# Output weights prepared block by block behind contexts, query weights prepared at projection borders, and a later start of the three-head query lead

## The chip, the cores and the metric

The kernel runs on one core of a Trainium2 chip. A core has five engines that run side by side, each with a queue of its own that it works off in order: TensorE (PE in the profile; PEld are its weight loads, which overlap its matmuls), VectorE (DVE), ScalarE (ACT), GpSimd (POOL) and SyncE (SP), which here only issues DMAs. Engines wait for one another through semaphores. The metric is the device time of one execution in microseconds (us); a kernel's time is the median of its runs.

## The reference

The input is x with 4 sequences of 512 tokens and 1024 features, all in fp32. Four residual layers follow, each after a layer norm: a mixing across sequences, a linear layer with routed low-rank additions, a low-rank attention with 32 heads, and a linear layer with sequence-routed low-rank additions. The change concerns only the attention, which for one sequence is

```
q   = rmsnorm(x @ wq_a.T) @ wq_b.T            -> 32 heads x (64 plain + 64 rotary)
ckv, k_pe = split(x @ wkv_a.T)                -> 64 shared values, 64 rotary ones
k_nope, v = split(rmsnorm(ckv) @ wkv_b.T)     -> per head 64 and 128
scores = ([q_nope, rope(q_pe)] . [k_nope, rope(k_pe)]) * scale, causal
out = softmax(scores) @ v                     -> 32 heads x 128
y   = out @ wo.T                              -> 1024
x   = x + y
```

## The kernel before

**Stages.** By the profile's time, the first two layers fill 0 to 330 us, the low-rank projections of the attention 330 to 421 us, the heads 421 to 1496 us, and the last projection and the last layer the rest. The change lies in the heads.

**fp32 products.** The kernel splits each fp32 operand of a large product into a high part (a rounded copy, made by ACT or DVE) and a low part (the remainder, a subtraction by DVE or POOL) and adds three products: low by high, high by low, high by high (`matmul3`, lines 150 to 152). An operand thus always exists as a pair h, l.

**Units.** The keys and values are kept in the 64-wide shared form, so that the per-head key and value weights are folded into the query weights and the output weights. A unit u is one head of one sequence: 128 units, in 4 groups of 8 heads; within a group the 4 sequences follow one another, 8 heads each. One pass of the loop at line 1215 handles these things of different units:

- `query` of unit u+3: six 512-column matmuls into the one PSUM bank `psq`; `rotate_query`: ACT copies it to `qf` (L729), DVE makes the two rotated halves (L731, L732), POOL multiplies and adds (L733, L734);
- `split_query` of unit u+1: DVE rounds the high part `qh` (L741), POOL makes the low part `ql` (L742);
- `scores` of unit u: four pieces of 512, 384, 256 and 128 columns; the first three need `qh` and `ql`. DVE masks each and takes a minimum (L919), ACT takes the exponential (L922);
- `turn` of unit u-1: ten transposes of the probabilities on PE (L943), evicted by ACT and DVE (L945);
- `context` of units u-3 and u-2, in every second pass: sixteen profiled matmuls into `psv` (L959). Their results have 64 rows, so that two of them run side by side on PE;
- a few steps of a filler (the counts `per`): for the first sequence of a group `prepare_output`, otherwise `project` of the sequence before.

**Output weights.** Per group, `prepare_output` folds `wo` with the value weights. A block n is one pair of heads; its two halves of 512 columns are two PSUM tiles `poa` and `pob` (one buffer each), each made by two 64-row matmuls (L1069) from `slotC`, one buffer that `fetch_output` loads anew for each block (L1047, L1049). The projection runs as a two-by-two scheme of seven products (Strassen, in Winograd's form): of each two blocks seven operands are made, b11, b21, b22 and t1 to t4, each with a high part by ACT (`high`, L1083) and a low part by DVE or POOL (`low`, L1092 and L1089), with copies out of PSUM (`kept`, L1078) and differences (`less`, POOL L1096 or DVE L1099) in between. The copies lie in slices of the tile `raw`, of which there is one, shared with the loads of the query weights. Per group these are 24 operations on ACT, 16 on DVE and 6 on POOL. `issue_after` tells the scheduler to place a step behind a named instruction.

**Query weights.** A group has two sets, of four heads each. `fetch_query` loads the raw weights, in five DMAs on SP's queue, in the passes of heads 0 and 4 of a group's last sequence; `prepare_query` (L683, L684, L688, L145, L146) makes the pairs from them: four matmuls in `pob`, two copies on ACT, one subtraction on DVE and one on POOL. It is called in the middle of a pass, for the first set at head 3 of that last sequence and for the second at head 0 of the next group:

```
if (b, i) == (NB - 1, 3) and g + 1 < NG:
    wqs[2 * g + 2] = prepare_query(wq_raw, pso, "pob")
if (b, i) == (0, 0) and g > 0:
    wqs[2 * g + 1] = prepare_query(wq_raw, pso, "pob")
if u + 3 < NU:
    query(u + 3, psq, "psq")
    rotate_query(u + 3)
```

**Order.** The program is written in the order above, and the tile framework's scheduler then merges the steps into one fixed queue per engine. At run time each queue is worked off in that order, whatever is ready.

## Time and profile before

| | us |
|---|---|
| median of three runs | 1746.12 |
| the three runs | 1748.56, 1744.06, 1746.12 |
| profiled execution | 1748.5 |
| its span in the profile | 1746.3 |
| PE busy | 1704.6 |
| DVE, ACT, POOL busy | 1305.6, 903.5, 925.3 |
| span, 437.7 to 521.5 (group 0's output weights) | 83.8, of which PE busy 81.5 |
| mean of one `high` (L1083), `low` on DVE (L1092), `low` on POOL (L1089) | 0.60, 0.69, 1.29 |
| mean of one L733 or L734 on POOL, one L742 | 1.29, 1.02 |

The profiled execution is the slowest of the three. The page gives busy times of each engine over the span; a row of the timeline gives a start, a duration, the engine, the line, what is written and read, and in brackets how long the engine had sat idle and what released it. Because matmuls are pipelined, the time between the starts of two matmuls is the price of the first, not its own duration.

### The profile page before, as it was taken

The page shows a single profiled execution, that of the slowest core. Times are in us where ns is not written, and L with a number is a line of the kernel's source. Part 1 is how long each engine was busy: PE and PEld are TensorE (multiplying, and loading weights), DVE is VectorE, ACT ScalarE, POOL GpSimd, SP SyncE. Part 2 cuts the span into 40 slices and gives each one's busy share as a digit, 9 for nine tenths or more (in the row PEclk, how much of TensorE's full clock was granted, in tenths as well). Part 3 has the DMA queues.
Part 4 walks back from the last instruction along what each step waited for, and adds up shares of the span by engine and source line. Part 5 has one row for each costly group of instructions (what it writes and reads, how often), then busy time and mean ns, then how long its engine had stood idle before and what let it go on. Part 6 is the DMA issues. An engine that isn't in the chain of part 4 may idle for free.

```text
span 1746.3 us, 31729 instructions
## 1 busy us (share of the span) xinstructions
PE 1704.6 (98%) x10536; PEld 1432.1 (82%) x10536; DVE 1305.6 (75%) x3494; ACT 903.5 (52%) x2316; POOL 925.3 (53%) x926
## 2 busy tenths in 40 slices
PE   7999999999999999999999999999999999999999
PEld 6899999998767777767787767778777877789998
DVE  7977885676877777787777677777778777687675
ACT  7422331365765565475555476555466555453332
POOL 0553541202666565666666656666556664675454
PEclk9999999999999999999999999999999999999999
DMA  5313543245324234353333353242344333853431
GB/s 194 134 42 116 183 161 114 89 137 166 103 92 140 97 108 148 98 175 113 113 126 105 113 183 116 97 148 94 130 159 156 108 101 121 308 199 123 138 110 68
DMA packets 131940, 228.17 MB, mean 131 GB/s; under 512 B 22272, under 2 KB 58752, under 8 KB 128448
## 3 DMA queue, kind: packets, MB, share of 16 engines
q1 hardware_dynamic: 131776, 226.13, 38.7%
q8 instruction: 84, 1.38, 0.3%
q14 instruction: 80, 0.66, 0.1%
HBM read 156.60 MB, written 71.83 MB: 131 GB/s over the span
## 4 chain that ended last, share of the span: by engine, by line
PE 85%; DVE 7%; DMA 3%; ACT 2%; POOL 2%; issue 2%; SPq 0%; DVEq 0%; ACTq 0%; POOLq 0%
PE psv L959 8%; PE pst L943 8%; PE pss L150 4%; PE po L150 4%; PE po L152 4%; PE po L151 4%; PE pss L151 4%; PE pss L152 4%; PE pob L150 3%; PE psq L150 3%; PE poa L150 3%; PE psq L151 3%; PE psq L152 3%; PE pob L152 3%; PE pob L151 3%; PE acc L150 3%
## 5 line engine op out<-in xcount | busy, mean ns | idle before, releaser
L922 ACT ACTIVATE p<-p,mn 128x512 f32<-128x512 f32 (+3 forms) x512 | 284.6, 558 | 218.6 <-DVE mn L919 214.3
L919 DVE CUSTOM_DVE_ANT_0 p<-pss,causal 128x512 f32<-128x512 f32 (+3 forms) x512 | 232.4, 486 | 29.1 <-PE pss L152 21.9
L733 POOL TENSOR_TENSOR qf<-qf,ropeT 64x512 f32<-64x512 f32 x128 | 164.5, 1285 | 167.1 <-ACT qf L729 165.1
L943 PE MATMUL pst<-ident,p 128*128 128x128 f32 x1280 | 186.1, 273 | 3.7 <-ACT pT L945 3.7
L734 POOL TENSOR_TENSOR qf<-qf,wA 64x512 f32<-64x512 f32 x128 | 164.5, 1285 | 31.2 <-DVE wA L732 24.8
L943 PEld LDWEIGHTS pst<-ident,p 128*128 128x128 f32 x1280 | 153.0, 141 | 31.1 <-ACT pT L945 8.2
L742 POOL TENSOR_TENSOR ql<-qf,qh 128x384 fp32r<-128x384 f32 x128 | 131.1, 1024 | 63.9 <-DVE qh L741 47.6
L994 POOL TENSOR_TENSOR cxl<-s,cxh 128x256 fp32r<-128x256 f32 x128 | 96.8, 764 | 119.0 <-ACT cxh L993 65.1
L945 ACT COPY pT<-pst 128x512 f32<-128x512 f32 x256 | 142.4, 578 | 23.3 <-PE pst L943 21.3
L150 PE MATMUL pss<-kT,ql 128*128 128x512 f32 (+2 forms) x384 | 144.0, 375 | 0.8 <-DVE mn L919 0.4
L150 PE MATMUL po<-w_h,hTl 128*128 128x384 f32 (+1 forms) x384 | 133.1, 347 | 0.8 <-DVE x L433 0.8
L151 PE MATMUL pss<-kT,qh 128*128 128x512 f32 (+2 forms) x384 | 131.5, 342 | 0.0
L152 PE MATMUL pss<-kT,qh 128*128 128x512 f32 (+2 forms) x384 | 130.4, 340 | 0.0
L152 PE MATMUL po<-w_h,hTh 128*128 128x384 f32 (+1 forms) x384 | 130.1, 339 | 0.0
L151 PE MATMUL po<-w_l,hTh 128*128 128x384 f32 (+1 forms) x384 | 129.7, 338 | 0.0
L945 DVE COPY pT<-pst 128x256 f32<-128x256 f32 x128 | 54.3, 424 | 94.2 <-PE pst L943 93.1
L729 ACT COPY qf<-psq 128x512 f32<-128x512 f32 x126 | 74.0, 587 | 71.7 <-PE psq L152 71.7
L731 DVE TENSOR_TENSOR wA<-psq,ropeT 32x512 f32<-32x512 f32 x126 | 87.7, 696 | 22.5 <-ACT qf L729 19.5
L994 POOL TENSOR_TENSOR cxl<-cx,cxh 128x256 fp32r<-128x256 f32 x96 | 73.7, 769 | 55.6 <-ACT cxh L993 53.1
L922 ACT ACTIVATION_READ_ACCUMULATOR p<-p,mn 128x1 f32 x512 | 96.9, 189 | 0.0
L150 PEld LDWEIGHTS pss<-kT,ql 128*128 128x128 f32 x384 | 72.6, 189 | 21.9 <-DVE mn L919 4.3
L732 DVE TENSOR_TENSOR wA<-psq,ropeT 32x512 f32<-32x512 f32 x126 | 87.0, 691 | 1.7
(511 smaller groups left out, 4979.1 us busy)
## 6 DMA issues: line engine op xcount, KB each, us to landing
xs<-x_d SPq DMA_DIRECT2D x128, 256.0 KB
x_d<-xs SPq DMA_DIRECT2D x128, 256.0 KB
slotC<-in_woT_dram SPq DMA_DIRECT2D x32, 512.0 KB
rb<-r_d SPq DMA_DIRECT2D x128, 128.0 KB
w_t<-raw SPq DMA_DIRECT2D x32, 288.0 KB
x<-in_x_dram SPq DMA_DIRECT2D x16, 512.0 KB
x_d<-x SPq DMA_DIRECT2D x32, 256.0 KB
slotA<-q_d SPq DMA_DIRECT2D x8, 1024.0 KB
```

Of the source, the lines that this page charges most:

```text
L150: T.matmul(ps, lhsT=al, rhs=bh, start=start, stop=False, **kw)
L151: T.matmul(ps, lhsT=ah, rhs=bl, start=False, stop=False, **kw)
L152: T.matmul(ps, lhsT=ah, rhs=bh, start=False, stop=stop, **kw)
L733: G.tensor_tensor(f[mid], f[mid], ropeT[mid, 0, :], ALU.mult)
L734: G.tensor_tensor(f[mid], f[mid], t2[mid], ALU.add)
L742: G.tensor_tensor(l, f[:, P:S], f32(h), ALU.subtract)
L919: turn_of[0] = V.tensor_tensor_reduce(out=to, in0=ps[:, 0:n], in1=causal[:, S - n : S], scale=1.0, scalar=-NEG, op0=ALU.add, op1=ALU.min, ...
L922: A.activation(to, to, AF.Exp, bias=mn[:, i : i + 1], scale=-1.0, accum_out=rs[:, i : i + 1])
L943: T.transpose(ps[:, w : w + P], p[:, OF[i] + j * P : OF[i] + (j + 1) * P], ident)
L945: copy(pT[:, AT[js[0]] : AT[js[0]] + w], ps[:, 0:w])
L959: T.matmul(ps[n * KVR : (n + 1) * KVR, S - w : S], lhsT=k[:, j, :], rhs=pTs[u + n][:, AT[j] : AT[j] + w], start=(j == 0), stop=(j == TPB - 1))
L994: G.tensor_tensor(l, src, f32(h), ALU.subtract)
```

## The change

**Blocks.** `block(n)` makes both halves of a block at once, in both PSUM tiles, and loads the next block after it. The 22 steps of a group are written anew as 24, six in the stretch from a block to the next within a pair and six behind it, with two more differences kept in the free slices 4 and 5 of `room`. `less` goes to POOL whenever both sources lie in SBUF. Group 0 has an order of its own: 20 operations on ACT, 8 on DVE and 14 on POOL, where later groups have 16, 14 and 8. The counts of filler steps per pass (`per`) change so that a block follows a context.

**Query weights.** `fetch_query`'s result goes to a list, and `project` prepares it at the start of each half of a projection, with the bank that this half does not yet use.

**Queries.** Up to unit `EXTRA` = 12, a pass makes `query(u + 2)`, not `query(u + 3)`, and `split_query(u + 1)` comes after the first steps of the scores. In pass 12 both queries, of units 14 and 15, are made; from then on the order is that of before.

```diff
@@ -1014,6 +1014,9 @@
                             splitter(cxp, HG // 4, "cx"))
             parts = [next(outs), next(outs)]
             for j in range(0, TPB, 2):
+                if fetched_q:
+                    n, fetched = fetched_q.pop(0)
+                    wqs[n] = prepare_query(fetched, pso, "po" + "ab"[(1 + j // 2) % 2])
                 at, xs, banks = {}, {}, {}
                 for t, k in ((0, 0), (1, 1), (0, 1), (1, 0)):
                     at[t, k] = x_d[b * TPB + j + t][k]
@@ -1060,15 +1063,16 @@
             prs = [c + k for c in range(HG // 4) for k in (0, HG // 4)]
             po, tiles = {}, {}
 
-            def block(n, half, at):
+            def block(n):
                 nonlocal fetched
                 wo, wv = fetched
-                po[at] = pso.tile([P, 512], F32, name="po" + at)
                 with ExitStack() if g else tc.issue_after(scored[0].ins):
-                    for k in range(2):
-                        T.matmul(po[at][k * KVR : (k + 1) * KVR, :], lhsT=wv[:, k, :],
-                                 rhs=wo[k][:, half * 512 : half * 512 + 512], start=True, stop=True)
-                if half and n + 1 < len(prs):
+                    for half, at in enumerate("ab"):
+                        po[at] = pso.tile([P, 512], F32, name="po" + at)
+                        for k in range(2):
+                            T.matmul(po[at][k * KVR : (k + 1) * KVR, :], lhsT=wv[:, k, :],
+                                     rhs=wo[k][:, half * 512 : half * 512 + 512], start=True, stop=True)
+                if n + 1 < len(prs):
                     fetched = fetch_output(g, prs[n + 1])
 
             def src(at):
@@ -1092,89 +1096,66 @@
                     V.tensor_tensor(l, src(at), f32(h), ALU.subtract)
 
             def less(to, a0, a1):
-                if not {to, a0, a1} & set(po):
+                if not {a0, a1} & set(po):
                     G.tensor_tensor(src(to), src(a0), src(a1), ALU.subtract)
                     return
                 with tc.issue_after(turn_of[0].ins):
                     V.tensor_tensor(src(to), src(a0), src(a1), ALU.subtract)
 
             def steps():
-                block(0, 0, "a")
-                yield
-                kept(0, "a")
-                high("b11", "a")
-                block(0, 1, "b")
-                yield
-                low("b11", "a")
-                kept(1, "b")
-                yield
-                less("b", "b", 0)
-                block(1, 0, "a")
-                yield
-                high("t1", "b")
-                kept(0, "b")
-                kept(2, "a")
-                high("b21", "a")
-                yield
-                low("t1", "b")
-                low("b21", "a")
-                block(1, 1, "b")
-                yield
-                high("b22", "b")
-                kept(3, "b")
-                yield
-                low("b22", 3)
-                less("b", "b", 0)
-                block(2, 0, "a")
-                yield
-                high("t2", "b")
-                kept(5, "a")
-                less(3, 3, 1)
-                yield
-                low("t2", "b")
-                less("b", 2, "b")
-                high("b11", "a")
-                yield
-                high("t4", "b")
-                high("t3", 3)
-                low("b11", "a")
-                yield
-                low("t4", "b")
-                low("t3", 3)
-                block(2, 1, "a")
-                yield
-                kept(1, "a")
-                yield
-                less("a", "a", 5)
-                block(3, 0, "b")
-                yield
-                high("t1", "a")
-                kept(5, "a")
-                kept(2, "b")
-                high("b21", "b")
-                yield
-                low("t1", "a")
-                low("b21", "b")
-                block(3, 1, "a")
-                yield
-                high("b22", "a")
-                kept(3, "a")
-                yield
-                low("b22", 3)
-                less("a", "a", 5)
-                yield
-                high("t2", "a")
-                less(3, 3, 1)
-                yield
-                low("t2", "a")
-                less("a", 2, "a")
-                high("t3", 3)
-                yield
-                high("t4", "a")
-                low("t3", 3)
-                yield
-                low("t4", "a")
-                yield
+                for n in (0, 2):
+                    block(n)
+                    yield
+                    kept(1, "b")
+                    yield
+                    high("b11", "a")
+                    less(4, 1, "a")
+                    yield
+                    low("b11", "a")
+                    yield
+                    high("t1", 4)
+                    yield
+                    low("t1", 4)
+                    yield
+                    block(n + 1)
+                    yield
+                    if g == 0:
+                        kept(3, "b")
+                        less(5, "b", 4)
+                        high("b21", "a")
+                        yield
+                        kept(2, "a")
+                        high("b22", 3)
+                        low("b21", "a")
+                        yield
+                        high("t2", 5)
+                        low("b22", 3)
+                        less(3, 3, 1)
+                        low("t2", 5)
+                        yield
+                        high("t3", 3)
+                        less(2, 2, 5)
+                        low("t3", 3)
+                        yield
+                    else:
+                        less(5, "b", 4)
+                        high("b22", "b")
+                        yield
+                        low("b22", "b")
+                        less(2, "a", 5)
+                        high("b21", "a")
+                        yield
+                        less(3, "b", 1)
+                        low("b21", "a")
+                        high("t2", 5)
+                        yield
+                        low("t2", 5)
+                        high("t3", 3)
+                        low("t3", 3)
+                        yield
+                    high("t4", 2)
+                    low("t4", 2)
+                    yield
 
             return steps()
 
@@ -1211,7 +1192,9 @@
                     nc.sync.dma_start(out=tiles[t][:, k * 512 : (k + 1) * 512], in_=x_d[2 * q + t][k])
 
         filler = None
+        fetched_q = []
         cx = None
+        EXTRA = 12
         for u in range(NU + 3):
 
 
@@ -1219,12 +1202,12 @@
             g, b = divmod(B, NB)
             if i == 0 and B > 0:
                 filler = project(*divmod(B - 1, NB))
-            per = ((4, 1, 0) if i % 2 else (1, 1, 0)) if b else (2 + (i < HG // 2 + 2), 2, 2) if i >= HG // 2 else (3, 3, 1)
+            per = ((4, 1, 0) if i % 2 else (1, 1, 0)) if b else (2, 2, 2) if i >= HG // 2 else (3, 3, 1)
             if B == 0:
-                per = (0, 1, 2)
+                per = (1, 1, 1)
             if b == 0 and i == (HG // 2 if g else 0) and g < NG:
                 filler = prepare_output(g, wo_raw)
-            if u + 1 < NU:
+            if EXTRA < u < NU - 1:
                 split_query(u + 1)
             sc = scores(u) if u < NU else iter(())
             tn = turn(u - 1) if 0 < u <= NU else iter(())
@@ -1234,10 +1217,11 @@
             advance(sc)
             advance(cx)
             advance(filler, per[0])
+            if u <= EXTRA:
+                split_query(u + 1)
 
             if u == 0:
                 query(2, psq, "psq")
-                rotate_query(2)
             advance(sc)
             advance(sc)
             advance(tn)
@@ -1245,15 +1229,18 @@
             advance(filler, per[1])
             if u < NU:
                 g, b, i = units[u]
-                if (b, i) == (NB - 1, 3) and g + 1 < NG:
-                    wqs[2 * g + 2] = prepare_query(wq_raw, pso, "pob")
-                if (b, i) == (0, 0) and g > 0:
-                    wqs[2 * g + 1] = prepare_query(wq_raw, pso, "pob")
-            if u + 3 < NU:
+            if 0 < u <= EXTRA:
+                query(u + 2, psq, "psq")
+            if u <= EXTRA:
+                rotate_query(u + 2)
+            if EXTRA < u < NU - 3:
                 query(u + 3, psq, "psq")
                 rotate_query(u + 3)
             advance(filler, per[2])
             advance(tn)
+            if u == EXTRA:
+                query(u + 3, psq, "psq")
+                rotate_query(u + 3)
             if u < NU:
                 g, b, i = units[u]
                 if i == 2 and u + HG < NU:
@@ -1262,7 +1249,8 @@
                 if b == 0 and i == 0:
                     wo_raw = fetch_output(g, 0)
                 if (b, i) in ((NB - 1, 0), (NB - 1, 4)) and g + 1 < NG:
-                    wq_raw = fetch_query(2 * g + 2 + i // 4)
+                    n = 2 * g + 2 + i // 4
+                    fetched_q.append((n, fetch_query(n)))
                 if (g, b) == (NG - 1, NB - 1) and i == 1:
                     late = raw()
                     hs = {0: [late[:, (t + 1) * D : (t + 2) * D] for t in range(2)]}
```

## The prediction

> **What bounds the kernel now.** I read, in this order, the busy line of the page, the groups of instructions, the waits of the tensor engine in the stretches that the change touches, and there the rows in order of time. A difference counts when it is over 0.3% (5.2 us); less can't be told from no change here. The busy line first:

> ```profile
> PE 1704.6 (98%) x10536; PEld 1432.1 (82%) x10536; DVE 1305.6 (75%) x3494; ACT 903.5 (52%) x2316; POOL 925.3 (53%) x926
> ```

> PE is busy 98% of the span, so time is lost only where PE gets more to do or waits; no other engine is near full over the span. PE's waits in group 0's output weights (437 to 522 us, where all of group 0's part of the change lies), and then in the same work of the later groups (700 to 1420 us):

> ```profile
> engine line waited for: us in total, times, longest us
> PE pst L943 <- ACT pT L945: 2.2, 1, 2.2
> ```

> ```profile
> PE pst L943 <- ACT pT L945: 1.5, 3, 0.5
> PE pob L150 <- POOL cxl L994: 0.9, 3, 0.3
> PE poa L1069 <- DMA slotC<-in_wv_dram: 0.6, 1, 0.6
> ```

> So there is 2.25 us to win in group 0, and 3.0 us over the three later groups, 1.0 each. What the first wait stands behind is seen in ACT's rows in order of time (start, duration):

> ```profile
> 492.92 0.62 ACT L1083 CAST t31h<-raw 128x512 fp32r<-128x512 f32 x1 [2.48 <-POOL raw L1096]
> 493.45 0.72 ACT L922 ACTIVATE p<-p,mn 128x512 f32<-128x512 f32 x1
> ```

> One ACT copy waited 2.48 us for one subtraction on POOL, and the exponentials of the next head, queued behind it, came late to the transposes. An output-weight operation thus costs time by standing in a queue ahead of something that the scores need. That is what to look for in the new order. The last rows are POOL's own, for one query in this stretch, and what lies around it:

> ```profile
> 479.61 1.01 POOL L742 TENSOR_TENSOR ql<-qf,qh 128x384 fp32r<-128x384 f32 x1 [2.49 <-DVE qh L741]
> 481.15 1.28 POOL L733 TENSOR_TENSOR qf<-qf,ropeT 64x512 f32<-64x512 f32 x1 [0.52 <-ACT qf L729]
> 482.58 1.29 POOL L734 TENSOR_TENSOR qf<-qf,wA 64x512 f32<-64x512 f32 x1 [0.16 <-DVE wA L732]
> 484.78 1.02 POOL L742 TENSOR_TENSOR ql<-qf,qh 128x384 fp32r<-128x384 f32 x1 [0.91 <-DVE qh L741]
> ```

> The last three are one query: its matmuls ended at 480.3, and its low part was there at 485.8, 5.5 us later, with only its own three POOL operations in the queue. Its head's first scores start at 493.6, 13 us after its matmuls, so nothing is lost before the change.

> **Part 1, blocks in both halves.** PE's instructions are the same set; only their order differs, from 437.7 to about 520 us and in three like stretches later. Rows give: a whole context (16 matmuls into 64 rows, side by side in pairs) 2.30 us (488.36 to 490.66); a context with two block halves in it 4.14 (458.76 to 462.90), so 1.84 for two halves; one half alone 1.01 to 1.08; the first pair of a split context alone 1.00 (498.49 to 499.49) and its rest 2.29. Group 0 before: five halves alone (5.05), two whole contexts (4.6), two with halves (4.14 + 4.20), one split (3.29), one more whole (2.30): 23.6 us. After: one whole context with both halves (4.0), five first pairs alone (5.0), three rests with both halves (12.0), two rests (4.6): 25.6. **+2.0 us**: blocks become cheaper, but three contexts more are cut in two. At each later group the same count gives +0.63 for the block stretch, -0.65 for a context that becomes whole, -0.1 for query weights behind a context: -0.1.

> Evictions in group 0: ACT 24 to 20 (0.60 us each), DVE 16 to 8 (0.69), POOL 6 to 14 (1.29). Later groups: ACT 24 to 16, DVE 16 to 14, POOL 6 to 8. ACT and DVE get lighter by 2.4 and 5.5 us, POOL heavier by 8 x 1.29 = 10.3 us in group 0's two pairs of blocks. POOL is the engine that also makes the queries. The 2.25 us wait goes: the subtraction that ACT waited for is a different one now, and no exponential stands right behind it: **-2.3**.

> **Part 2, query weights moved.** Per set: 4 matmuls (0.9 us of PE), two ACT copies (0.62, 0.58), one DVE (0.69) and one POOL operation (1.28). All move from inside heads 0 and 3 to the two starts of a projection's half. They stay beside PE work of several heads, and the sets are used no sooner than before; if that cover goes, PE waits up to the 3.2 us of their chain. Their five loads on SP's queue keep their place in the head loop, but now some stand ahead of the load for a block (512 KB x2, 5.7 us alone, wanted about 7 us after its issue): 0 to 1 us of wait. At each later group I take the old wait of 1.0, less the -0.1 of matmul order, less 0.4 for what may come back: **-0.7** each, bounds -1.1 and +0.9; times three, -2.1.

> **Part 3, the additional query in the thirteenth head.** In the first twelve heads the query is now made two heads ahead instead of three, so its low part has to be ready one head after its matmuls, not two. For the query of head 7 I follow the new queues with the rows above; zero is the end of the block of pair 1. PE: last scores of head 5 and eight transposes (1.5), six query matmuls to 2.95; then two transposes 0.2, first scores of head 6 1.2, three transposes 0.3, scores 0.4, five transposes 0.5, first pair of the context 1.1, query 8 with one score 1.7, two transposes 0.2: scores of head 7 are wanted at about 8.8, 5.8 us after the query. The bare chain needs 5.5. But POOL's order is now: low part of head 6's query, a subtraction, b22's low part, first rotation of query 7, a subtraction, t2's low part, t4's low part, and only then the second rotation and the low part of query 7. b22's high part leaves ACT at 4 to 4.9, behind two evictions and two exponentials; POOL then runs b22l to 5.8, rotation to 7.1, three more at 1.29 to 11.0, second rotation 12.3, DVE's high part 12.7, low part **13.7**, against 8.8: PE waits 4.9. If ACT is a microsecond sooner or my PE count short, 3.5; with everything late, 5.4. The lower end, no wait at all, would need the three extra operations to be done before the first rotation, which the queue excludes as long as they wait for ACT. I take **4.7 us**. The same order comes again for head 11's query: **2 x 4.7 = 9.4 us**. Queries 5 and 9, with one extra POOL operation ahead, come out even (0 to 0.5, taken as 0). Behind the waiting POOL operation stand the next query and a context's low part; both have a head's slack after the wait. DVE's high part of query 7 also holds the last mask of head 6 until 12.7, inside the same wait.

> A long wait costs the clock too. The windows show it after PE's one long idle before the heads (columns: length, busy of PE, weight loads, DVE, ACT, POOL, then the granted clock, DMA share, GB/s):

> ```profile
> 426.60:430.00 3.40, 0.95 (x4) 0.85 (x5) 1.76 (x4) 0.75 (x2) 3.11 (x3) 1.00 0.95 303
> 430.00:433.40 3.40, 3.02 (x9) 1.96 (x9) 2.09 (x9) 1.96 (x7) 0.50 (x2) 0.50 0.57 184
> 433.40:436.80 3.40, 3.40 (x13) 3.03 (x13) 1.90 (x5) 2.34 (x8) 2.11 (x2) 0.50 0.00 0
> ```

> After 2.68 us idle in a 3.4 us stretch PE ran at 0.50 for 6.8 us: 3.4 us lost. The wait of 2.25 us at 494 cost no clock. A wait of 4.7 us fills most of a stretch at any phase; one slow stretch costs 1.7, two cost 3.4. I take 1.7, since the second slow stretch above followed a first one with idle time in it: **2 x 1.7 = 3.4 us**, bounds 0 and 6.8.

> [...]

> **Sum.** 2.0 - 2.3 - 2.1 + 9.4 + 3.4 = +10.4 us. Against the profiled execution (1748.5; span 1746.3) that is 1758.9. The profiled execution is the slowest of the three and stands 2.4 above their median, so the median becomes **1756.5**.

> **Rivals.**
> (a) Not slower: POOL finds the extra low parts' inputs early (ACT gets b22 out 3 us sooner than I count), so the query's chain is in time and all old waits go. The price is 2.0 - 2.3 - 3 x 1.1 = -3.6: 1742.5. For it: ACT and DVE get lighter, and ACT's copies are what the chain starts with. Against: ACT's exponentials for one head take 2.2 us (493.45 to 495.64) and half of them stand ahead. It decides if query 7's low part is there within 5.8 us of its matmuls. With every old wait gone in group 0 and after, and a static gain at the three later groups twice mine, it would just pass 0.3%.
> (b) Small stalls: the query is late by 1 to 1.5 us twice and no clock drops: 2.0 - 2.3 - 2.1 + 2.5 = 0: 1746. This is also how it would look if the change did nothing measurable. For it: PE's pace in my count may be 5% fast, and late transposes give POOL time.
> (c) More: both waits cost two slow clock stretches each, and the later groups wait for a block's load: 10.4 + 3.4 + 3 x 1.6 = +18.6: 1764.7. For it: the window rows above; against: the block's load has 1.3 us to spare.

> **How the numbers follow.** My forecast 0.52, (a) 0.20, (b) 0.15, (c) 0.13. The forecast's own range is 1750 to 1762 (stalls 3.5 to 5.4, clock 0 to 5). The range to hold 8 in 10 reaches into (a) and to (c): 1742 to 1766. Faster by over 0.3% (under 1740.9) is half of (a), 0.10; within 0.3% the rest of (a), (b) and the low edge of the forecast, 0.28; slower 0.62.

> **What would show it.** In the changed kernel's profile: PE waits of 3 to 5 us before scores (weights from ql) near 472 and 505 us, released by POOL's L742; POOL's low parts (now in the function that makes them) between the two rotations; a granted clock of 0.50 right after; the 2.25 us wait gone; PE's own 64-row work up by 2 us in group 0; and no wait over 1 us in the later groups. I am wrong if POOL's queue is clear when the query matmuls end, or if the wait moves to DVE's masks.

## The result and the profile after

The changed kernel takes 1760.0 us (median of 4 runs, 1758.2 to 1760.2) against 1745.8 us before (1744.1 to 1748.6): a ratio of 1.0074, 95% interval 1.006 to 1.0089. It is 14.2 us slower, where +10.4 was forecast. The profiled execution's span is 1758.3 us.

The busy line of the changed kernel's page, which answers to the one shown of before:

```profile
PE 1708.8 (97%) x10536; PEld 1436.0 (82%) x10536; DVE 1298.3 (74%) x3480; ACT 891.6 (51%) x2288; POOL 942.7 (54%) x940
```

PE has the same 10536 matmuls by the profile's count and is busy 4.2 us longer; ACT and DVE have less to do and POOL more, as counted. PE's waits in group 0's output weights (437 to 540 us; the columns are the total in us, how many, and the longest):

```profile
PE pss L150 <- POOL ql L742: 9.2, 4, 4.2
```

and in the later groups (700 to 1420 us):

```profile
PE pss L150 <- DVE mn L919: 2.9, 6, 0.8
PE pst L943 <- ACT pT L945: 1.5, 3, 0.5
PE pob L150 <- POOL cxl L994: 0.9, 3, 0.3
```

The wait of 2.25 us behind ACT is gone; in its place PE waits four times for a query's low part on POOL, 0.40, 4.22, 0.40 and 4.19 us (heads 5, 7, 9 and 11). In the later groups the wait for a load is gone, the two other old waits have stayed, and six new waits for masks have come.

POOL's rows in order of time around the first long wait (start, duration; L1093 makes low parts, L1100 subtractions, L733 and L734 the two rotations of query 7, L742 its low part):

```profile
463.23 1.29 POOL L1093 TENSOR_TENSOR b220l<-raw,b220h 128x512 fp32r<-128x512 f32 x1
464.60 1.28 POOL L733 TENSOR_TENSOR qf<-qf,ropeT 64x512 f32<-64x512 f32 x1
465.96 1.28 POOL L1100 TENSOR_TENSOR raw<-raw 128x512 f32<-128x512 f32 x1
467.19 1.29 POOL L1093 TENSOR_TENSOR t20l<-raw,t20h 128x512 fp32r<-128x512 f32 x1
468.44 1.26 POOL L1093 TENSOR_TENSOR t40l<-raw,t40h 128x512 fp32r<-128x512 f32 x1
469.78 1.26 POOL L734 TENSOR_TENSOR qf<-qf,wA 64x512 f32<-64x512 f32 x1
471.58 1.00 POOL L742 TENSOR_TENSOR ql<-qf,qh 128x384 fp32r<-128x384 f32 x1 [0.54 <-DVE qh L741]
```

Three operations stand between the two rotations, and POOL has no gap over 0.1 us from 463.2 to 471.0: the query is late because of what is queued, not because POOL waits. PE's row that waited, from PE's rows:

```profile
472.63 0.80 PE L150 MATMUL pss<-kT,ql 128*128 128x512 f32 x1 [4.22 <-POOL ql L742]
```

The windows from this wait on, and then those around the second long wait (length, busy of PE, weight loads, DVE, ACT and POOL, granted clock, DMA share, GB/s), show the slow clock:

```profile
468.40:472.60 4.20, 0.01 (x1) 0.00 (x0) 0.91 (x4) 0.93 (x4) 3.56 (x4) 0.90 0.00 1
472.60:476.00 3.40, 3.37 (x9) 2.24 (x11) 1.64 (x4) 1.68 (x5) 3.09 (x3) 0.50 0.00 0
476.00:479.40 3.40, 3.40 (x18) 2.11 (x16) 1.17 (x4) 0.71 (x2) 1.47 (x2) 0.62 0.00 0
```

```profile
505.90:509.30 3.40, 0.51 (x2) 0.47 (x3) 0.90 (x4) 1.46 (x5) 2.63 (x3) 1.00 0.00 0
509.30:512.70 3.40, 3.40 (x12) 1.97 (x13) 2.56 (x5) 1.14 (x4) 3.16 (x5) 0.50 0.29 84
```

To see where the time lies I cut each trace at the first score matmul of certain heads. In a stretch, "idle" is the time without any matmul, "clock" is half of the time that PE worked at a granted clock of 0.50 (in the changed kernel a 512-column matmul took 0.43 us from start to start there, at 473.2, and 0.23 at 1.00, at 488.4; counting half is my estimate from these), and "work" is what is left, that is PE's work at full clock. Each row is one profiled execution. For heads 2 to 15, the stretch with all of group 0's output weights (us):

| kernel | length | idle | clock | work |
|---|---|---|---|---|
| before | 94.6 | 2.3 | 0 | 92.4 |
| changed | 110.7 | 9.2 | 4.7 | 96.9 |
| changed, lead of three (e1) | 104.8 | 7.0 | 4.3 | 93.5 |
| before, lead of two (e2) | 99.2 | 3.1 | 0 | 96.1 |
| changed, t4 on DVE (e3) | 109.1 | 7.8 | 4.5 | 96.9 |
| changed, t4 and t2 on DVE (e4) | 105.6 | 5.2 | 3.4 | 97.0 |
| changed, t4, t2 and a subtraction on DVE (e5) | 102.4 | 4.7 | 0 | 97.7 |
| the same, lead of three (e5b) | 95.9 | 2.2 | 0 | 93.7 |
| changed, POOL reordered (e14) | 103.0 | 5.4 | 0 | 97.6 |

With a lead of two, this stretch holds one query more (14 for 13; 1.4 us of six matmuls at 0.235 from start to start) that would otherwise lie before head 2. The later groups' stretches, heads 15 to 47, 47 to 79 and 79 to 111:

| kernel | 15 to 47 | 47 to 79 | 79 to 111 | sum |
|---|---|---|---|---|
| before | 271.1 | 271.2 | 271.8 | 814.1 |
| changed | 271.5 | 271.7 | 271.7 | 814.9 |
| changed, query weights at their old places (e7) | 273.0 | 273.0 | 273.4 | 819.4 |
| before, query weights at their new places (e8) | 269.9 | 269.9 | 270.1 | 809.9 |

Between the two profiled spans lie 12.0 us: +16.1 in heads 2 to 15, +0.8 in the later groups, -2.5 in heads 0 to 2 (one slow stretch of the clock fewer, 1.6, and the moved query), -2.2 before head 0, where nothing is changed and eleven other profiles spread by 2 us, and -0.3 behind the heads.

### The profile page after: what moved, and what is told of

The parts are those of the page before. It is cut to its first block, busy times and chain, and to the rows that moved or that the text cites. A ratio compares the mean times of both kernels' runs of the same rounds, so it can differ in the third digit from the quotient of the medians.

```text
span 1758.3 us, 31697 instructions
## 1 busy us (share of the span) xinstructions
PE 1708.8 (97%) x10536; PEld 1436.0 (82%) x10536; DVE 1298.3 (74%) x3480; ACT 891.6 (51%) x2288; POOL 942.7 (54%) x940
## 4 chain that ended last, share of the span: by engine, by line
PE 86%; DVE 6%; POOL 3%; DMA 3%; ACT 1%; issue 1%; SPq 0%; DVEq 0%; POOLq 0%; ACTq 0%
PE psv L959 8%; PE pst L943 7%; PE po L150 4%; PE po L152 4%; PE po L151 4%; PE pss L150 4%; PE pss L151 4%; PE pss L152 3%; PE pob L150 3%; PE poa L150 3%; PE psq L152 3%; PE psq L151 3%; PE psq L150 3%; PE pob L152 3%; PE pob L151 3%; PE poa L152 3%
## 5 line engine op out<-in xcount | busy, mean ns | idle before, releaser
L922 ACT ACTIVATE p<-p,mn 128x512 f32<-128x512 f32 (+3 forms) x512 | 284.1, 557 | 237.7 <-DVE mn L919 237.3
L733 POOL TENSOR_TENSOR qf<-qf,ropeT 64x512 f32<-64x512 f32 x128 | 164.5, 1285 | 168.9 <-ACT qf L729 164.9
L943 PE MATMUL pst<-ident,p 128*128 128x128 f32 x1280 | 186.2, 273 | 1.5 <-ACT pT L945 1.5
L734 POOL TENSOR_TENSOR qf<-qf,wA 64x512 f32<-64x512 f32 x128 | 165.1, 1290 | 29.0 <-DVE wA L732 22.5
L943 PEld LDWEIGHTS pst<-ident,p 128*128 128x128 f32 x1280 | 152.5, 141 | 29.5 <-ACT pT L945 6.3
L742 POOL TENSOR_TENSOR ql<-qf,qh 128x384 fp32r<-128x384 f32 x128 | 130.4, 1019 | 66.7 <-DVE qh L741 37.5
L945 ACT COPY pT<-pst 128x512 f32<-128x512 f32 x256 | 142.2, 577 | 41.4 <-PE pst L943 40.3
L994 POOL TENSOR_TENSOR cxl<-s,cxh 128x256 fp32r<-128x256 f32 x128 | 96.9, 764 | 118.5 <-ACT cxh L993 59.5
L150 PE MATMUL pss<-kT,ql 128*128 128x512 f32 (+2 forms) x384 | 143.7, 374 | 12.9 <-POOL ql L742 9.2
L150 PE MATMUL po<-w_h,hTl 128*128 128x384 f32 (+1 forms) x384 | 133.0, 346 | 0.4 <-DVE x L433 0.4
L945 DVE COPY pT<-pst 128x256 f32<-128x256 f32 x128 | 54.3, 424 | 98.9 <-PE pst L943 98.4
L729 ACT COPY qf<-psq 128x512 f32<-128x512 f32 x126 | 73.7, 585 | 74.9 <-PE psq L152 73.1
L731 DVE TENSOR_TENSOR wA<-psq,ropeT 32x512 f32<-32x512 f32 x126 | 87.6, 695 | 26.2 <-ACT qf L729 22.8
L150 PEld LDWEIGHTS pss<-kT,ql 128*128 128x128 f32 x384 | 72.6, 189 | 39.0 <-POOL ql L742 10.7
L994 POOL TENSOR_TENSOR cxl<-cx,cxh 128x256 fp32r<-128x256 f32 x96 | 72.9, 759 | 45.6 <-ACT cxh L993 42.5
L922 ACT ACTIVATION_READ_ACCUMULATOR p<-p,mn 128x1 f32 x512 | 96.2, 188 | 0.0
L1039 DVE TENSOR_TENSOR xs<-xs,poa 128x512 f32<-128x512 f32 x105 | 71.4, 680 | 23.6 <-PE poa L152 23.3
```

The source lines that it names most:

```text
L150: T.matmul(ps, lhsT=al, rhs=bh, start=start, stop=False, **kw)
L733: G.tensor_tensor(f[mid], f[mid], ropeT[mid, 0, :], ALU.mult)
L734: G.tensor_tensor(f[mid], f[mid], t2[mid], ALU.add)
L742: G.tensor_tensor(l, f[:, P:S], f32(h), ALU.subtract)
L922: A.activation(to, to, AF.Exp, bias=mn[:, i : i + 1], scale=-1.0, accum_out=rs[:, i : i + 1])
L943: T.transpose(ps[:, w : w + P], p[:, OF[i] + j * P : OF[i] + (j + 1) * P], ident)
```

## The experiments

The theory is the prediction's: group 0's new POOL operations stand ahead of a query that a lead of two heads makes urgent. The rivals are that the lead itself costs it, that POOL has simply too much to do, and that the order of the blocks costs on PE. The runs were made in three sittings, in which the kernel before took 1746.9, 1746.4 and 1747.5 us. The changed kernel's 1760.0 was not taken again beside them, so that differences from it can be off by 1 to 2 us.

**e1: the lead of three heads again.**

```diff
-        EXTRA = 12
+        EXTRA = 0
```

> The changed kernel with the lead of three heads from the first head on (the third part undone, blocks and query weights as changed). Theory (the queries of heads 7 and 11 are late because POOL stands in the extra low parts and the lead is only one head long): both waits of 4.2 us before the scores go, and with them the slow clock (4.7 us) and the three waits of 0.3 to 0.4 us in group 0's first heads: 1760.0 - 8.4 - 4.7 - 0.8 = 1746. The POOL order of subtraction, t2's and t4's low part between a query's two rotations stays (now query 8's), and costs nothing. Rival (the order of the blocks and evictions itself costs): the waits move to another line and the time stays over 1755.

Measured: 1756.6 us against 1746.9 before, 1.0057 (1.0042 to 1.0072). Only 3.4 us came back. PE's waits in heads 0 to 15 now have another name:

```profile
PE pss L150 <- DVE mn L919: 6.9, 2, 3.5
```

The rows of DVE and of PE at that place say why:

```profile
472.87 0.36 DVE L741 CAST qh<-qf 128x384 fp32r<-128x384 f32 x1 [5.47 <-POOL qf L734]
473.14 0.28 DVE L919 CUSTOM_DVE_ANT_0 p<-pss,causal 128x128 f32<-128x128 f32 x1
473.69 0.68 DVE L919 CUSTOM_DVE_ANT_0 p<-pss,causal 128x512 f32<-128x512 f32 x1
```

```profile
473.49 0.69 PE L150 MATMUL pss<-kT,ql 128*128 128x384 f32 x1 [3.50 <-DVE mn L919]
```

POOL has the same three operations between the two rotations, now of query 8. That query is not needed until one head later. But DVE's rounding of it (`qh`, L741) stands in DVE's queue ahead of the masks of the heads that run now, and waits 5.47 us for the second rotation; the score banks are not emptied, and PE stops. So the rival expectation held: the wait moved to another line and the time stayed over 1755. The lead gave little slack, 3.5 us of wait for 4.2, because a queue hands the lateness on. The POOL order was the cause all the same, as e5b and e14 below show.

**e2: the lead of two heads alone, on the kernel before** (the third part of the diff, nothing else).

> The kernel before with only the third part (lead of two heads in the first twelve). Theory: POOL has only b22's low part and one subtraction ahead of query 7's rotations and t3's low part between them, so that the query comes 2.6 us earlier than in the changed kernel: PE waits 0 to 2 us per pair of blocks, no slow clock; 1745.8 + 0 to 4: 1746 to 1750. Rival (a lead of two heads costs it all, whatever else POOL does): 1757 or more.

Measured: 1747.8 us against 1746.9, 1.0006 (0.9997 to 1.0016). PE's waits in the same stretch:

```profile
PE pst L943 <- ACT pT L945: 1.8, 1, 1.8
PE pss L150 <- POOL ql L742: 1.1, 2, 0.7
```

As the theory had it: the query is late by 0.75 us, no clock is lost here, and between the medians the lead of two alone costs 0.9 us, which is not clear of nothing (the interval is -0.5 to +2.8). The table shows 3.7 us more PE work in this stretch, of which 1.4 is the moved query; one context more is cut in two, and the rest is not explained. Over heads 0 to 15 the two profiles differ by more than the medians: 2.6 us of work and 1.3 of idle time more, against 1.7 less lost to the clock in heads 0 to 2.

**e3, e4, e5: the operations between the rotations taken off POOL one by one.**

```diff
-                        less(3, 3, 1)
-                        low("t2", 5)
+                        less(3, 3, 1, False)    # e5
+                        low("t2", 5, False)     # e4, e5
...
-                    low("t4", 2)
+                    low("t4", 2, g > 0)         # e3, e4, e5
```

`False` sends the operation to DVE.

> The changed kernel with t4's low part of group 0 on DVE. Theory: one POOL operation of 1.26 to 1.29 us less between the query's rotations, so both waits fall from 4.2 to 2.9 us; the slow clock after them gets shorter or goes (2.25 us cost no clock, 2.68 us did): 1760.0 - 2.6 and up to 4.7 more: 1753 to 1757.5. Rival (the wait is set by ACT or DVE, POOL's order is only what came last): waits and time unchanged, 1759 to 1761.

> The changed kernel with t4's and t2's low parts of group 0 on DVE. Theory: both waits fall to 1.6 us and no slow clock follows: 1760.0 - 5.2 - 4.7 = 1750. Rival (ACT or DVE sets the wait): 1758 to 1761. Between the two for the clock: if it stays slow after 1.6 us, 1755.

> The changed kernel with t4's and t2's low parts and the second subtraction of group 0 on DVE: nothing of the output weights stands between query 7's rotations on POOL any more, with a lead of two heads still. Theory (it is POOL's operations between the two rotations, not the length of the lead): waits of 0.5 us or less at heads 7 and 11, no slow clock: 1760.0 - 7.4 - 4.7 = 1748. Rival (a lead of one head is too short whatever stands there): waits of 1.5 us and more, 1753 or more.

Measured: 1757.3, 1756.5 and 1752.3 us; before took 1746.9 beside the first two (1.0064, 1.0049 to 1.0079; 1.0053, 1.0037 to 1.007) and 1746.4 beside the third (1.0044, 1.0029 to 1.006). PE's waits, one line of each:

```profile
PE pss L150 <- POOL ql L742: 7.8, 4, 3.5
```

```profile
PE pss L150 <- POOL ql L742: 5.0, 4, 2.1
```

```profile
PE pss L150 <- POOL ql L742: 4.7, 4, 1.9
```

With three, two, one and no operation between the rotations, the longest wait is 4.2, 3.5, 2.1 and 1.9 us. The direction is the theory's, the size of the steps is not (1.3 each was expected): 1.9 us remain where 0.5 or less was. By time, e3 lies at the upper end of its range, e4 6.5 us over its theory and just under its rival, and e5 is nearer to its rival (waits of 1.5 us and more, 1753) than to its theory. What remains in e5 is t3's low part, which now stands ahead of query 7's low part on POOL, and DVE, whose added work got longer there (1.69 us for one subtraction; see the last section). Time followed less than the wait in e4: its waits of 2.1 us still cost two slow stretches of the clock, 3.4 us; in e5's profile those of 1.9 cost none. But that profile is the fastest of e5's four runs (1750.3 to 1757.1 us), and the other three have a lower mean granted clock, 0.997 to 0.999 against 1.000.

**e5b: the same with the lead of three** (e5 and e1 together).

> The same with the lead of three heads. Theory: 1746 to 1748, within 1 us of the kernel with the lead of two, since both have POOL's queue clear. Rival (the lead matters by itself): 3 us and more below it.

Measured: 1748.2 us against 1746.4, 1.0006 (0.9997 to 1.0015), 4.1 below e5; the longest wait is 1.1 us, for a mask on DVE. So the rival held by its number: with nothing of the output weights between the rotations, a lead of two still costs about 4 us under the new blocks, half of it in waits (idle 4.7 against 2.2) and half in PE's order. It isn't the lead alone, since in e5 t3's low part still stands ahead of the query that is wanted next; on the kernel before, the lead cost less (e2). The two roughly add up: against the changed kernel the lead alone gives 3.4 us (e1), POOL's operations alone 7.7 (e5), both 11.8.

**e14: all operations kept on POOL, but behind a query's low part.**

```diff
-                    G.tensor_tensor(l, src(at), f32(h), ALU.subtract)
+                    (behind if kind in ("b22", "t1") else much_later)(l, src(at), f32(h))
...
+            for to, a0, a1 in soon + (late_ if u in (8, 11) else []):
+                with tc.issue_after(halved[0].ins):
+                    G.tensor_tensor(to, a0, a1, ALU.subtract)
```

`halved[0]` is the last query's low part; `behind` and `much_later` fill the two lists for group 0, which are issued after `split_query` of the passes that follow.

> The changed kernel (lead of two heads) with all of group 0's low parts and subtractions still on POOL, as many as in the changed kernel, but placed behind the low part of a query instead of between its two rotations; PE's order is that of the changed kernel. Theory (the place in POOL's queue costs, not its load and not the lead): waits before the scores of heads 7 and 11 under 1 us, no slow clock: 1760.0 - 7 - 4.7 = 1748. Rival (POOL has too much to do in these heads): a wait of 3 us or more turns up elsewhere, 1754 or more. Between: ACT's high parts of t3 and t4 now wait for subtractions that come later, and exponentials stand behind them: 1 to 2 us a pair, 1750 to 1752.

Measured: 1751.8 us against 1747.5, 1.0031 (1.0019 to 1.0043). PE's waits:

```profile
PE pob L150 <- POOL cxl L996: 2.8, 1, 2.8
PE pst L945 <- DVE ri L884: 1.7, 1, 1.7
PE pss L150 <- POOL ql L744: 0.7, 2, 0.5
```

The same number of operations on the same engine in another order: the waits for a query fall from 9.2 to 0.7 us, no clock is lost from 437 to 545 us, and the kernel is some 8 us faster than the changed one. So it was the place in the queue, not POOL's load. The time lies in the range of the between-case, but not for its reason (high parts late on ACT). The operations pushed back make other things late. The first projection waits 2.8 us for an operand that stands behind three of them in POOL's queue, close to the 3 us that the rival named. The wait of 1.7 us at head 9 comes, as the rows read, by e1's path: two low parts stand ahead of a rotation on POOL, and DVE's rounding of that query waits for it and stands ahead of two masks, with exponentials and copies behind them on ACT:

```profile
492.58 0.36 DVE L743 CAST qh<-qf 128x384 fp32r<-128x384 f32 x1 [3.11 <-POOL qf L734]
```

**e7 and e8: the query weights.** In e7 the changed kernel prepares them where they were before; in e8 the kernel before gets only this part of the diff.

```diff
-                if fetched_q:
-                    n, fetched = fetched_q.pop(0)
-                    wqs[n] = prepare_query(fetched, pso, "po" + "ab"[(1 + j // 2) % 2])
...
+                if (b, i) in ((NB - 1, 3), (0, 0)) and fetched_q:
+                    n, f_ = fetched_q.pop(0)
+                    wqs[n] = prepare_query(f_, pso, "pob")
```

> The changed kernel with the query weights prepared where they were before (the second part undone). Theory: the second part is hidden work, so 1759 to 1761; heads 16 to 127 as long as in the changed kernel within 0.5 us. Rival (the moved preparation makes the new waits of 0.3 to 0.8 us on DVE's masks at the three later groups): those six waits go, 1757 to 1758.

> The kernel before with only the second part (query weights prepared at the starts of a projection's halves). Theory (the query weights' move makes one context more per group whole on PE, as undoing it under the new blocks cost 1.1 us of PE work per group): 1.1 less at each of three groups: 1746.4 - 3.3 = 1743. Rival (hidden anyway): 1746 to 1747.

Measured: e7 1764.0 us against 1746.4, 1.0103 (1.0089 to 1.0116), 4.0 slower than the changed kernel; e8 1741.8 us against 1747.5, 0.9971 (0.9962 to 0.998). Neither expectation of e7 held: undoing this part cost 4 us. e8 is 5.7 us faster than the kernel before, more than its theory's 3.3. PE's rows at one border show what it does. Before (the weights' four matmuls, which the profile counts as eight, then the next context):

```profile
694.00 1.05 PE L688 MATMUL pob<-raw 128*128 128x128 f32 x8
695.50 2.15 PE L959 MATMUL psv<-pT,slotA 128*64 128x512 f32 x10
699.17 0.86 PE L959 MATMUL psv<-pT,slotA 128*64 128x256 f32 x6
```

e8:

```profile
665.65 2.37 PE L959 MATMUL psv<-pT,slotB 128*64 128x512 f32 x16
667.95 1.16 PE L688 MATMUL poa<-raw 128*128 128x128 f32 x8
```

```profile
698.77 2.38 PE L959 MATMUL psv<-pT,slotA 128*64 128x512 f32 x16
```

In the middle of a pass, the weights' matmuls came just ahead of the next context, and that context was cut in two by the six matmuls of a query (10 and 6 matmuls, 2.15 + 0.86 = 3.0 us against 2.37 whole); behind a context they leave the next one whole. In each later group, two contexts are cut in the kernel before and one in e8, three in e7 and two in the changed kernel: each time the weights' old place goes with one cut more. In e8 PE's work falls by 1.1 to 1.2 us per group, and with 0.1 to 0.5 less idle this is 4.2 us over the three groups. Of the 1.1 us, counted from start to start in the first of them, 0.6 is the context; 0.7 less is in the matmuls of queries and scores, and 0.2 more in the weights' own. The other 1.5 us between the medians lie outside these stretches and are not explained. This part of the change is a gain, and the rest of the change costs the later groups 5.3 us (819.4 against 814.1).

**e9 and e15: what ACT waited for in the kernel before.** All subtractions of the output weights on DVE; e15 is e8 and this.

```diff
-                if not {to, a0, a1} & set(po):
+                if False:
```

> The kernel before with all subtractions of the output weights on DVE instead of POOL. Theory (ACT's high part of t3 waited for POOL's subtraction, and the exponentials behind it): the wait of 2.25 us in group 0 and the three of 0.49 later go: 1746.9 - 3.7 = 1743. Rival (the 0.7 us that DVE gets ahead of the masks cost as much): 1746 to 1748.

> The kernel before with the second part, and with all subtractions of the output weights on DVE. Theory: the gain of the second part alone and the little that the subtractions bring add up: 1742 to 1743. Rival (on DVE the subtractions stand before masks, and PE's order in group 0 has two contexts more that are cut): 1744 to 1746.

Measured: e9 1745.9 us against 1746.4, 0.9996 (0.9987 to 1.0005); e15 1739.9 us against 1747.5, 0.9962 (0.9949 to 0.9976). In e9 the wait of 2.25 us and the three of 0.49 are gone, as the theory said, but PE's work in heads 2 to 15 is 1.4 us longer (93.7 against 92.4) and smaller waits have come: nothing is left that can be measured, as the rival said. e15 is faster than both kernels; its interval overlaps with e8's, so what the subtractions add to the query weights is not settled. Both expectations of e15 were too high.

## Why the prediction was right, point by point

The forecast was 1756.5 us, slower, with 1742 to 1766 around it; 1760.0 lies inside, 3.5 us over the forecast, and the mechanism that it named is in the rows.

- **The late query (Part 3, 2 x 4.7 us).** Right in place and in kind: 4.22 us at head 7 and 4.19 at head 11, at 468.4 and 504.6 us, behind the very three operations that were listed, and 0.40 each at heads 5 and 9 (0 to 0.5 was said). From the same zero, the scores were wanted at 9.0 instead of 8.8 (the pieces listed in the step add up to 8.6), and the low part was there at 13.2 instead of 13.7. It was wrong in what it laid this to. The step read a lead of three as slack ("nothing is lost"); e1 shows 3.5 us of wait with that slack, through DVE's queue, where `qh` stands ahead of the masks. I had traced that `qh` held "the last mask of head 6 until 12.7" and taken it for part of the same wait; it is a path of its own.
- **The clock (2 x 1.7 us).** 4.7 us lost instead of 3.4: after the first wait the clock was slow for 6.8 us, after the second for 3.4. The bounds of 0 to 6.8 held. The step saw that a second slow stretch followed a first one with idle time in it, but didn't apply this to its own wait, which reached 0.88 us into the first slow stretch (see the last section). It also read 2.68 us as the idle time of a 3.4 us stretch; that is the whole gap, and the row shown has 2.45.
- **PE's order in group 0 (+2.0).** Mis-sized: work over heads 0 to 15 grew by about 3.3 us (102.6 to 105.9). Four contexts more are cut in two, not three as the step says (its own count has one before and five after). Under the new blocks alone (e1) the growth is 1.4 us (104.0); the lead of two brought the rest.
- **The old wait (-2.3).** Gone, as said.
- **Query weights (Part 2, hidden).** Mis-sized. Part 2 has the move itself as hidden; Part 1 has -0.65 per later group for a context that becomes whole and -0.1 for the weights' place, and by the count of cut contexts above these two are the same move. Together that is -0.75 per group; e8 has -1.1 to -1.2 of work and -0.1 to -0.5 of idle time, -4.2 us over the three groups, and between the medians the move is worth 5.7 us alone and 4.0 under the new blocks. What was left out are the query and score matmuls around the cut.
- **Later groups (-0.7 each).** They came out at +0.4, +0.4 and 0.0. Work fell by 0.4 each (0.1 was counted), but idle rose by 0.8, 0.9 and 0.4. The step let 0.6 of each group's old 1.0 us of waits go; only the one wait for a load went. The waits for masks (0.28 and 0.56 to 0.78 us) were not foreseen; new waits for a block's load did not come, and no wait is over 1 us, as said.

The sum of these as measured (order, old wait, later groups, the two long waits, the two short ones, the clock): 3.3 - 2.3 + 0.8 + 8.4 + 0.8 + 4.7 = +15.7, against +10.4. The order, the later groups and the clock were 1.3, 2.9 and 1.3 us too low; the late query, the largest term, was right within 0.2 (9.2 for 9.4). In the two profiles 1.6 goes off for one slow stretch fewer in heads 0 to 2, and 2.5 for the stages before and behind the heads: 11.6, against 12.0 between the spans. That these 4.1 us, which no step forecast, bring the profiles nearer to the forecast is luck. By parts, the blocks with their order on POOL cost most, the shorter lead 3.4 under them (e1), and the query weights gave 4 back (e7).

The rival of the other side (a) failed where it was said to decide: the low part came 10.2 us after its matmuls (462.3 to 472.6), not within 5.8. Its own price, -3.6 us, also lies within the 0.3% (5.2 us), so that half of its chance could not count as faster.

## What to carry to other kernels

An operation that is moved to a less busy engine is paid for by what stands behind it in that engine's queue (here PE waited 4.2 us for a query behind three operations of 1.3 us each), and a longer lead helps little while another engine's queue has the late operand ahead of urgent work (here 3.5 us of wait stayed, through DVE's queue): follow the late result through every queue that reads it. Before costing a moved step by its own operations, look at what it stood between: where the weights' matmuls stood cost 1.1 to 1.2 us of PE's time, and they themselves take 0.8 to 0.9. When a part of a change looks like housekeeping, run it alone; here it was the only one of the three parts that paid.

## What the runs showed of the hardware

| kernel | window from | idle in it | slow stretch behind it | idle in that stretch's first 3.41 us |
|---|---|---|---|---|
| before | 47.7 | 1.98 | 3.41 | 0.00 |
| before | 426.6 | 2.46 | 6.83 | 0.38 |
| changed | 424.0 | 2.68 | 3.41 | 0.17 |
| changed | 468.3 | 3.33 | 6.83 | 0.88 |
| changed | 505.9 | 2.91 | 3.41 | 0.00 |

All other windows at full speed held less idle time, at most 1.72 us in the kernel before (at 1508.6) and 1.71 in the changed one (at 48.5). The changed kernel's first long wait reached 0.88 us into the slow window, and the next window was slow too; its second ended before the slow window. The place of the idle time on the grid counted, too: the wait of 2.25 us of the kernel before lay as 0.85 and 1.40 in two windows and cost nothing, while 1.98 in the one window at 47.7 cost 1.7 us. What lies between 1.72 and 1.98 us these two profiles don't show.

**Some of DVE's operations ended just after one of POOL.** In e5 one subtraction per pair of blocks, of two operands in SBUF, moved to DVE. DVE's row, and POOL's at that time; then the same kind of step in e9, with POOL idle:

```profile
464.21 1.69 DVE L1103 TENSOR_TENSOR raw<-raw 128x512 f32<-128x512 f32 x1
```

```profile
464.07 1.28 POOL L734 TENSOR_TENSOR qf<-qf,wA 64x512 f32<-64x512 f32 x1
```

```profile
461.07 0.69 DVE L1099 TENSOR_TENSOR raw<-raw 128x512 f32<-128x512 f32 x1 [0.34 <-POOL b220l L1089]
```

DVE took 1.69 us, 0.55 beyond POOL's end. The second such step of e5 took 1.59 us. Two low parts on DVE in e5 show the same: t2's, begun at 465.82 with POOL idle, took 0.68 us; t4's, begun at 467.24 during a POOL operation, took 1.26 and ended 0.54 us after that one. In the kernel before, DVE's rounding of a query (L741, a copy from SBUF to SBUF) took 0.31 to 0.36 us in all 64 cases where it began with POOL idle; in the 64 where it began during a POOL operation, it ended 0.2 to 0.3 us after that one, up to 0.74 in all (1.04 in the changed kernel). It may be a part of why moving work from POOL to DVE freed less than its duration; that part was not measured alone.
